# Weights of a tuned attention and feed-forward kernel placed at multiples of 512 bytes

## The chip, the cores and the metric

The kernel runs on one core of one Trainium2 chip. Its time is the device time of one execution in microseconds, taken as the median of several runs. On a core, TensorE multiplies matrices (PE in the profile, and PEld for the loading of its standing operand), VectorE (DVE), ScalarE (ACT) and GpSimd (POOL) work element by element, and SyncE (SP) mostly starts DMAs. SBUF, the memory that all of them work in, has 128 partitions; an address here is a byte offset inside a partition, the same in all 128. TensorE writes its results to PSUM, in 8 banks of 2048 bytes a partition.

## What is computed

8192 tokens (4 sequences of 2048) with 256 features each pass one layer: gated linear attention inside chunks of 32 tokens, a layer norm, a feed-forward part with integer weights, and a second layer norm.

```python
Q, K, V = x @ W_q.T, x @ W_k.T, x @ W_v.T
decay = sigmoid(log_decay[0])
mask = where(diff >= 0, decay ** diff, 0)         # 32 x 32, diff = row - column
S = einsum('bncd,bnkd->bnck', Qc, Kc) * mask      # inside each chunk of 32 tokens
O = einsum('bnck,bnkd->bncd', S, Vc).reshape(B, T, D)
out = sigmoid(x @ W_g.T) * O @ W_o.T + x
h = layernorm(x + out)
f = (silu(h @ (w_gate/127).T) * (h @ (w_up/127).T)) @ (w_down/127).T   # 256 -> 768 -> 256
y = layernorm(h + f)
```

## The kernel before

The tokens are worked on in 16 blocks of 512. W_q and W_k are first multiplied into one matrix m, so that a score is a product of x·m with x. The work is spread as a pipeline over the loop of line 1103: while one block is in its feed-forward part, the next ones are in attention. The order of the instructions on each engine is written out by hand: `in_turn` (line 115) keeps an instruction at its place in the program's order.

TensorE is fed by two kinds of products. In one kind the result has its features on the partitions: the weight is the **standing** operand (128 rows by 128 columns, loaded into the array beforehand) and 512 tokens stream past as the **moving** operand. In the other kind the result has its tokens on the partitions: 128 tokens stand, and a weight of 256 columns moves.

To get near float32 accuracy from quicker formats, numbers are split. In the attention products (lines 442 to 542) a weight and a token tile each come in three parts, `hi`, `lo` and `gap`, all in the format fp32r, and one product becomes three: hi with hi and lo with lo, then, after ScalarE has scaled the bank (line 533), gap with gap. `feature_major` (the matmul of line 492) makes the gate's and y's products this way, p_g and p_y: weights wg and m stand. `token_major` (line 514) makes p_v and p_o: weights wv and wo move. In the feed-forward part (`ffn_up`, line 870, matmul at line 881) the integer weights fg and fu stand in two exact copies, fp32r (hi) and fp16 (lo), against the two parts of the normed tokens, hT_hi and hT_lo. In its second half the parts of the hidden values, u_hi and u_lo, stand, and the weight fd moves (line 736; 955 and 1315 for the last blocks). The very last block's up products are partly done in two halves of 256 columns. Plain float32 products are used in the first block (lines 578, 599, 620, 769) and throughout for the chunk scores (line 654) and the values (line 690, where the masked scores sT move past v).

Where a tile lies follows from its pool. `tile_pool` calls take space in the order in which they are written, each pool gives space to its tags in the order of their first use, and each tag is rounded up to a multiple of 32 bytes. 16512 bytes in front are taken by the program. Then come the pools `const` (weights, masks and other things that stay), `setup`, `xin`, `work`, `norm`, `moved`, `acts`, `sums`, `small`, and last `tiny`, which holds tiles of one or a few columns. Before the change the first tile of const is `top`, 36 bytes rounded to 64, and in the middle of const stand `diff` and `chunk_mask` with 128 bytes each. The places of the tiles that TensorE reads are these, worked out from the sizes and the order:

| tiles | start before | past a multiple of 512 |
|---|---|---|
| wg, wv, wq, wk, wo (2048 each; wg, wv, wo later hold their gap parts, wq and wk hold m's hi and lo) | 16576 to 24768 | 192 |
| ident, m (m's gap) | 26816, 27328 | 192 |
| sT_0, sT_1 | 29632, 30656 | 448 |
| wg_hi, wg_lo, wv_hi, wv_lo, wo_hi, wo_lo | 31680 to 41920 | 448 |
| fg_hi, fg_lo, fu_hi, fu_lo, fd_hi, fd_lo | 43968 to 68544 | 448 |
| all tiles of tokens (xT, yT, v, hT, u, x and go parts) | from 73216 on | 0 |

Chunks inside a tile lie a multiple of 512 bytes apart, except in fg_lo and fu_lo, where 128 columns of fp16 are 256 bytes.

Of the kernel before, what the change touches and what calls it, by code (L numbers as in the profile page):

```python
# [47 lines left out]
F32 = mybir.dt.float32  # L48
F32R = mybir.dt.float32r
F16 = mybir.dt.float16  # L50
I32 = mybir.dt.int32
# [3 lines left out]
P = 128  # L55
CHUNK = 32
# [3 lines left out]
NG = TB // P  # L60
# [16 lines left out]
def kernel(  # L77
# [20 lines left out]
    NB = NT // TB  # L98
    assert NB > 3

    const = ctx.enter_context(tc.tile_pool(name="const", bufs=1))
    setup = ctx.enter_context(tc.tile_pool(name="setup", bufs=2))
    xin = ctx.enter_context(tc.tile_pool(name="xin", bufs=2))
# [8 lines left out]
    tiny = ctx.enter_context(tc.tile_pool(name="tiny", bufs=1))  # L112
    psum = ctx.enter_context(tc.tile_pool(name="psum", bufs=8, space=bass.MemoryType.PSUM))

    def in_turn(ins):
        tc.keep_in_program_order(ins)

    def bank(name):
        return psum.tile([P, TB], F32, tag="ps", name=name)
# [33 lines left out]


    n_pieces = sum(w.shape[0] * w.shape[1] // (P * TB) for w in (ffn_gT, ffn_uT, ffn_dT))
    top = const.tile([P, n_pieces], F32, tag="top", name="top")
    decay = tiny.tile([P, 1], F32, tag="decay", name="decay")
    xTs, xns = {}, {}
    wg = load_w(nc.scalar, w_gT, "wg", pieces=KD)
    xTs[0] = load_xT(0, pieces=KD)  # L160
# [43 lines left out]

    ident = const.tile([P, P], F32, tag="ident", name="ident")
    make_identity(nc, ident)
    eps = tiny.tile([P, 1], F32, tag="eps", name="eps")
    nc.vector.memset(eps, EPS)
    half = tiny.tile([P, NG], F32, tag="half", name="half")
    nc.vector.memset(half, -0.5)  # L210


# [16 lines left out]

    diff = const.tile([P, CHUNK], I32, tag="diff", name="diff")
    for g in range(P // CHUNK):
        nc.gpsimd.iota(
            diff[g * CHUNK : (g + 1) * CHUNK, :],
# [1 line left out]
            base=0,  # L237
            channel_multiplier=-1,
        )
    chunk_mask = const.tile([P, CHUNK], F32, tag="chunk_mask", name="chunk_mask")  # L240
    nc.vector.tensor_scalar(chunk_mask, diff, 0.0, None, ALU.is_ge)
    table = tiny.tile([P, 1], F32, tag="table", name="table")
    in_turn(nc.scalar.activation(table, eps, AF.Sigmoid))
    bits = []
    for i in range(CHUNK.bit_length() - 1):
# [13 lines left out]
    def make_mask():  # L259
        in_turn(nc.scalar.activation(decay, decay, AF.Sigmoid))  # L260
        power = decay
        for i, (bit, factor) in enumerate(bits):
            in_turn(
                nc.vector.scalar_tensor_tensor(factor, bit, power, factor, ALU.mult, ALU.add)
            )
            in_turn(nc.vector.tensor_tensor(chunk_mask, chunk_mask, factor, ALU.mult))
            if i < len(bits) - 1:
                square = tiny.tile([P, 1], F32, tag=f"power_{i}", name=f"power_{i}")
                in_turn(nc.vector.tensor_tensor(square, power, power, ALU.mult))
                power = square  # L270

# [31 lines left out]

    def wide_counter():

        wide = const.tile([P, top.shape[1]], F32, tag="wide", name="wide")
        in_turn(nc.vector.tensor_scalar(wide, top, EXACT, None, ALU.is_gt))
        ones = tiny.tile([P, 1], F32, tag="ones", name="ones")
        nc.vector.memset(ones, 1.0)

        def count_wide():
            pw = bank("pw")[:1, : top.shape[1]]
            in_turn(nc.tensor.matmul(pw, lhsT=ones, rhs=wide, start=True, stop=True))
            count = tiny.tile([1, 1], F32, tag="count", name="count")
            in_turn(nc.vector.tensor_reduce(count, pw, mybir.AxisListType.X, ALU.add))
            return count

        return count_wide
# [687 lines left out]

    weight_parts(wg, "wg", ("wg_hi", "wg_lo"))
    make_mask()
    back_to_silu()
    sg, gate = attn_gate(0)  # L1010
# [59 lines left out]
    y_rest()  # L1070
    look_up(range(6, n_pieces))
    count_wide = wide_counter()
    gate = g_rest(hold=True)
    hs[1], out_rest = split_out(1, go_parts)
    hTs[0] = transpose_h(0, hs[0])
    count = count_wide()
    n_wide_early = tiny.tile([1, 1], I32, tag="n_wide_early", name="n_wide_early")
    in_turn(nc.vector.tensor_copy(n_wide_early, count))
    gate()
    x_parts, x_gaps = token_parts(xTs[3], "x_3")  # L1080
# [414 lines left out]
        nc.gpsimd.dma_start(out[tokens, :], r)  # L1495


    n_wide = tiny.tile([1, 1], I32, tag="n_wide", name="n_wide")
    in_turn(nc.vector.tensor_copy(n_wide, count))
    of_others = loaded(n_wide, [e for e in mybir.ALL_ENGINES if e != mybir.EngineType.SP])  # L1500
    wide_any = bass.RuntimeValue.of_register_unchecked(
# [71 lines left out]
```

## Time and profile before

| | us |
|---|---|
| three runs | 487.17, 487.68, 488.32; median 487.68 |
| the profiled execution | 488.06 |
| its span, first to last instruction | 486.5 |
| granted TensorE clock over the span | 0.998 of full speed |
| TensorE busy (PE) | 480.3, 4760 instructions |
| loading of standing operands (PEld) | 381.5, 4760 instructions |
| ScalarE, VectorE, GpSimd busy | 374.6, 338.1, 281.1 |
| landing of the first weight, which the first product waits for | 3.36 |

The profile's groups give a line of the kernel, an engine, an operation, its tiles as out<-in, and its shape; for a matmul the first tile after the arrow is the moving one, the second the standing one. After the bar stand the busy time in us and the mean duration of one in ns. The view of the chain gives, in order of time, a start in us, a length in us, and what ran, with a count. The list of one tile gives the least, the median and the largest duration in ns. The view of waits gives who waited for whom: us in total, times, the longest.

### The profile page before, as it was taken

The page shows a single profiled execution, that of the slowest core. Times are in us where ns is not written, and L with a number is a line of the kernel's source. Part 1 is how long each engine was busy: PE and PEld are TensorE (multiplying, and loading weights), DVE is VectorE, ACT ScalarE, POOL GpSimd, SP SyncE. Part 2 cuts the span into 40 slices and gives each one's busy share as a digit, 9 for nine tenths or more (in the row PEclk, how much of TensorE's full clock was granted, in tenths as well). Part 3 has the DMA queues.
Part 4 walks back from the last instruction along what each step waited for, and adds up shares of the span by engine and source line. Part 5 has one row for each costly group of instructions (what it writes and reads, how often), then busy time and mean ns, then how long its engine had stood idle before and what let it go on. Part 6 is the DMA issues. An engine that isn't in the chain of part 4 may idle for free.

```text
span 486.5 us, 12289 instructions
## 1 busy us (share of the span) xinstructions
PE 480.3 (99%) x4760; PEld 381.5 (78%) x4760; DVE 338.1 (69%) x795; ACT 374.6 (77%) x699; POOL 281.1 (58%) x285
## 2 busy tenths in 40 slices
PE   9999999999999999999999999999999999999995
PEld 5788787887868878687887868878687787868685
DVE  4587958777676875757777676875757777667656
ACT  4778788687887878788787887878788787786845
POOL 3835755655745556465555745656465555657764
PEclk9999999999999999999999999999999999999999
DMA  8630321221413114131311313123131211103002
GB/s 256 229 101 25 104 71 49 49 80 36 125 33 113 44 51 126 31 101 52 108 60 38 127 32 112 45 65 110 26 106 53 80 44 37 54 20 113 32 16 85
DMA packets 43323, 36.99 MB, mean 76 GB/s; under 512 B 4864, under 2 KB 39168, under 8 KB 43264
## 3 DMA queue, kind: packets, MB, share of 16 engines
q1 hardware_dynamic: 42144, 35.28, 23.6%
q10 hardware_dynamic: 1120, 0.92, 0.6%
q8 instruction: 38, 0.62, 0.6%
q14 instruction: 21, 0.17, 0.1%
HBM read 20.45 MB, written 8.39 MB: 59 GB/s over the span
## 4 chain that ended last, share of the span: by engine, by line
PE 98%; DMA 1%; DVE 0%; ACT 0%; issue 0%
PE fg L881 18%; PE fu L881 18%; PE fdn L736 15%; PE p_o L514 9%; PE p_v L514 9%; PE p_y L492 9%; PE p_g L492 9%; PE po L690 4%; PE ps L654 2%; PE fdn L955 2%; PE fdn L1315 1%; PE pg L578 1%; PE pa L769 1%; PE pv L620 1%; PE py L599 1%; DMA wg<-in_w_gT_dram 1%
## 5 line engine op out<-in xcount | busy, mean ns | idle before, releaser
L907 POOL TENSOR_TENSOR u_lo<-u,u_hi 128x512 f16<-128x512 f32 (+1 forms) x98 | 129.6, 1328 | 95.2 <-ACT u_hi L906 94.2
L901 DVE SCALAR_TENSOR_TENSOR u<-fu,s 128x512 f32<-128x512 f32 (+1 forms) x98 | 66.2, 675 | 83.6 <-ACT s L890 81.4
L890 ACT ACTIVATE s<-fg 128x512 f32<-128x512 f32 (+1 forms) x98 | 57.4, 586 | 47.5 <-PE fg L881 47.5
L906 ACT CAST u_hi<-u 128x512 fp32r<-128x512 f32 (+1 forms) x98 | 59.3, 605 | 32.8 <-DVE u L901 32.8
L881 PE MATMUL fg<-hT_hi,fg_hi 128*128 128x512 f32 (+1 forms) x196 | 72.0, 449 | 0.0
L881 PE MATMUL fu<-hT_hi,fu_hi 128*128 128x512 f32 (+1 forms) x196 | 60.2, 389 | 0.0
L881 PE MATMUL fg<-hT_lo,fg_lo 128*128 128x512 f16 (+1 forms) x196 | 58.2, 379 | 0.0
L881 PE MATMUL fu<-hT_lo,fu_lo 128*128 128x512 f16 (+1 forms) x196 | 57.4, 375 | 0.0
L473 POOL TENSOR_TENSOR go_lo<-goT,go_hi 128x512 fp32r<-128x512 f32 x30 | 44.6, 1507 | 18.1 <-ACT go_hi L472 18.1
L479 DVE SCALAR_TENSOR_TENSOR go_gap<-go_hi,goT 128x512 fp32r<-128x512 f32 x30 | 48.1, 1644 | 0.8 <-ACT go_hi L472 0.7
L473 POOL TENSOR_TENSOR x_lo<-xT,x_hi 128x512 fp32r<-128x512 f32 x30 | 37.8, 1281 | 15.5 <-ACT x_hi L472 15.5
L736 PE MATMUL fdn<-fd_hi,u_hi 128*128 128x256 f32 x312 | 45.0, 287 | 0.0
L881 PEld LDWEIGHTS fg<-hT_hi,fg_hi 128*128 128x128 f32 x196 | 35.6, 189 | 10.2
L881 PEld LDWEIGHTS fu<-hT_hi,fu_hi 128*128 128x128 f32 x196 | 36.5, 188 | 8.1
L790 DVE TENSOR_TENSOR h<-p_o,x 128x512 f32<-128x512 f32 x30 | 19.3, 685 | 32.0 <-PE p_o L514 28.2
L736 PEld LDWEIGHTS fdn<-fd_hi,u_hi 128*128 128x128 f32 x312 | 39.3, 189 | 0.3
L736 PE MATMUL fdn<-fd_lo,u_lo 128*128 128x256 f16 x312 | 38.6, 273 | 0.0
L858 POOL TENSOR_TENSOR hT_lo<-hT,hT_hi 128x512 f16<-128x512 f32 x28 | 35.4, 1287 | 4.2 <-ACT hT_hi L857 4.2
L881 PEld LDWEIGHTS <-fu_lo 128*128 128x128 f16 x196 | 19.2, 98 | 22.2
L736 PEld LDWEIGHTS <-u_lo 128*128 128x128 f16 x312 | 28.4, 98 | 4.0
L426 ACT ACTIVATE h<-h,shift_h,scale_h 128x256 f32<-128x256 f32 x52 | 27.0, 590 | 1.6 <-DVE shift_h L389 0.8
L881 PEld LDWEIGHTS <-fg_lo 128*128 128x128 f16 x196 | 13.2, 98 | 19.0 <-issue 12.8
(175 smaller groups left out, 1040.2 us busy)
## 6 DMA issues: line engine op xcount, KB each, us to landing
x<-in_x_dram SPq DMA_DIRECT2D x16, 512.0 KB, 3.8
xT<-in_xT_dram SPq DMA_DIRECT2D x15, 512.0 KB, 4.3
hT<-sq SPq DMA_DIRECT2D x224, 32.0 KB, 1.9
out_dram<-r SPq DMA_DIRECT2D x13, 512.0 KB, 3.2
out_dram<-r SPq DMA_DIRECT2D x7, 128.0 KB, 1.7
fg_int<-in_ffn_gT_dram SPq DMA_DIRECT2D x3, 256.0 KB, 7.3
fu_int<-in_ffn_uT_dram SPq DMA_DIRECT2D x3, 256.0 KB, 6.4
fd_int<-in_ffn_dT_dram SPq DMA_DIRECT2D x3, 256.0 KB, 5.5
```

The costliest lines, as they stand in the source:

```text
L426: nc.scalar.activation(r[:, g, :], r[:, g, :], AF.Identity, bias=shift[:, g : g + 1], scale=scale[:, g : g + 1],)
L473: in_turn(nc.gpsimd.tensor_tensor(lo[:, k, :], t[:, k, :], whole, ALU.subtract))
L479: nc.vector.scalar_tensor_tensor(gap[:, k, :], whole, -WHOLE, t[:, k, :], ALU.mult, ALU.add)
L492: nc.tensor.matmul(pb, lhsT=a[kind][:, k, i * P : (i + 1) * P], rhs=b[kind][:, k, :], start=kind + k == 0, stop=True, skip_group_check=True,)
L514: nc.tensor.matmul(pb[:, j * D : (j + 1) * D], lhsT=b[kind][:, k, g * P : (g + 1) * P], rhs=a[kind][:, k, :], start=kind + k + j == 0, sto ...
L736: product = nc.tensor.matmul(pb[:, j * D : (j + 1) * D], lhsT=part[:, g * P : (g + 1) * P], rhs=w, start=(i == 0), stop=(i == len(terms) - 1),
L858: nc.gpsimd.tensor_tensor(in_order[1], whole, in_order[0].bitcast(F32), ALU.subtract)
L881: product = nc.tensor.matmul(pb, lhsT=w[kind][:, dc, hc * P : (hc + 1) * P], rhs=hT[kind][:, dc, cols], start=(kind == kinds[0] and dc == ...
L890: in_turn(nc.scalar.activation(s, pg, AF.Silu, scale=SCALE / H_UP))
L901: nc.vector.scalar_tensor_tensor(u, pu, U_UP / H_UP, s, ALU.mult, ALU.mult)
L906: in_steady_turn(nc.scalar.copy(hi, u))
L907: in_steady_turn(nc.gpsimd.tensor_tensor(lo, u, hi.bitcast(F32), ALU.subtract))
```

## The change

One more pool, `lead`, is opened in front of `const`. The twelve tiles of at most 16 bytes that were in `tiny` (decay, eps, half, table, four powers, ones, count, n_wide_early, n_wide) are taken from `lead`. The four small tiles of const whose sizes are no multiple of 512 (top, diff, chunk_mask, wide) are taken from `tiny`, behind all other pools. No instruction, size or order is changed.

```diff
+    lead = ctx.enter_context(tc.tile_pool(name="lead", bufs=1))
     const = ctx.enter_context(tc.tile_pool(name="const", bufs=1))
...
-    top = const.tile([P, n_pieces], F32, tag="top", name="top")
-    decay = tiny.tile([P, 1], F32, tag="decay", name="decay")
+    top = tiny.tile([P, n_pieces], F32, tag="top", name="top")
+    decay = lead.tile([P, 1], F32, tag="decay", name="decay")
...
-    eps = tiny.tile([P, 1], F32, tag="eps", name="eps")
+    eps = lead.tile([P, 1], F32, tag="eps", name="eps")
...
-    half = tiny.tile([P, NG], F32, tag="half", name="half")
+    half = lead.tile([P, NG], F32, tag="half", name="half")
...
-    diff = const.tile([P, CHUNK], I32, tag="diff", name="diff")
+    diff = tiny.tile([P, CHUNK], I32, tag="diff", name="diff")
...
-    chunk_mask = const.tile([P, CHUNK], F32, tag="chunk_mask", name="chunk_mask")
+    chunk_mask = tiny.tile([P, CHUNK], F32, tag="chunk_mask", name="chunk_mask")
...
-    table = tiny.tile([P, 1], F32, tag="table", name="table")
+    table = lead.tile([P, 1], F32, tag="table", name="table")
...
-                square = tiny.tile([P, 1], F32, tag=f"power_{i}", name=f"power_{i}")
+                square = lead.tile([P, 1], F32, tag=f"power_{i}", name=f"power_{i}")
...
-        wide = const.tile([P, top.shape[1]], F32, tag="wide", name="wide")
+        wide = tiny.tile([P, top.shape[1]], F32, tag="wide", name="wide")
...
-        ones = tiny.tile([P, 1], F32, tag="ones", name="ones")
+        ones = lead.tile([P, 1], F32, tag="ones", name="ones")
...
-            count = tiny.tile([1, 1], F32, tag="count", name="count")
+            count = lead.tile([1, 1], F32, tag="count", name="count")
...
-    n_wide_early = tiny.tile([1, 1], I32, tag="n_wide_early", name="n_wide_early")
+    n_wide_early = lead.tile([1, 1], I32, tag="n_wide_early", name="n_wide_early")
...
-    n_wide = tiny.tile([1, 1], I32, tag="n_wide", name="n_wide")
+    n_wide = lead.tile([1, 1], I32, tag="n_wide", name="n_wide")
```

## Prediction

> **What bounds the kernel now.** I read the page first: the share of each engine, then the chain that ended last, then the waits. TensorE is busy from end to end at the full granted clock, the chain lies on it, and no multiplication waits except the first warm-up one.
>
> ```profile
> span 486.5 us, 12289 instructions
> PE 480.3 (99%) x4760; PEld 381.5 (78%) x4760; DVE 338.1 (69%) x795; ACT 374.6 (77%) x699; POOL 281.1 (58%) x285
> ...
> PEclk9999999999999999999999999999999999999999
> ...
> PE 98%; DMA 1%; DVE 0%; ACT 0%; issue 0%
> ```
>
> ```profile
> PE pi L197 <- PEq L1558: 1.0, 1, 1.0
> ```
>
> So time changes only if a multiplication (PE) or a weight load (PEld) takes another time, or if something that is hidden today comes out. The other engines wait for TensorE or for each other; those waits cost nothing.
>
> Busy time of TensorE does not tell its pace, since matmuls overlap in their pipeline. The chain of waits does: there a piece is the distance from its first start to the next piece's start, so the piece divided by its count is the pace.
>
> ```profile
> 19.79 1.88 PE p_v L514 x16
> ...
> 61.32 1.82 PE p_v L514 x16
> ...
> 90.74 1.84 PE p_v L514 x16
> 92.58 1.83 PE p_g L492 x8
> ...
> 97.15 1.84 PE p_o L514 x16
> ...
> 100.89 5.43 PE fdn L736 x48
> ...
> 130.05 5.47 PE fdn L736 x48
> ```
>
> The two fdn lines say that one block of 512 tokens takes 29.16 us (130.05 less 100.89). The p_g line gives 1.83/8 = 229 ns for an fp32r multiplication of 512 columns; p_v and p_o at 1.84/16 give 115 ns for 256 columns. The reader should note the first three lines: the same sixteen instructions on the same addresses took 1.88, 1.82 and 1.84 us, that is 117.5, 113.8 and 115 ns each. There are two paces for one and the same instruction, and the block that it stands in, not its address, goes with which one it gets.
>
> **What the change moves, and by how much.** No instruction, wait, queue or DMA is added, removed or moved; only byte offsets within a partition change. In front of the const pool 16512 bytes are taken. Before, `top` (36 bytes, rounded to 64) stands there, so wg, wv, wq, wk, wo, ident and m start at 192 past a multiple of 512; their space is reused for the gap parts and for m's hi and lo. Behind `diff` and `chunk_mask` (128 bytes each) everything stands at 448: sT, wg_hi to wo_lo, and the hi and lo of fg, fu and fd. After, twelve tiles of 32 bytes stand in front: 16512 + 384 = 16896 = 33 x 512. With diff, chunk_mask, top and wide gone to the back, every const tile is a multiple of 512 long and starts at 0. The pools behind them start at 71680 as before and the tokens' tiles were at 0 already, so they do not move. So 192 and 448 become 0, for weights, and nothing else changes that TensorE reads in the loop but sT (448 to 0).
>
> **Standing weights (line 492, and 881).** Does a load at 0 take another time than one at 448 or 192? The rows already hold both: in the products over features the standing operand is a weight, in those over tokens (736) it is a token tile at 0.
>
> ```profile
> L736 PEld LDWEIGHTS fdn<-fd_hi,u_hi 128*128 128x128 f32 x312 | 39.3, 189 | 0.3
> L881 PEld LDWEIGHTS fu<-hT_hi,fu_hi 128*128 128x128 f32 x196 | 36.5, 188 | 8.1
> L881 PEld LDWEIGHTS fg<-hT_hi,fg_hi 128*128 128x128 f32 x196 | 35.6, 189 | 10.2
> L736 PEld LDWEIGHTS <-u_lo 128*128 128x128 f16 x312 | 28.4, 98 | 4.0
> L881 PEld LDWEIGHTS <-fu_lo 128*128 128x128 f16 x196 | 19.2, 98 | 22.2
> ...
> L492 PEld LDWEIGHTS p_y<-x_hi,m_hi 128*128 128x128 f32 x60 | 11.0, 188 | 2.3
> ```
>
> u_hi at 0 takes 189 ns, fg_hi and fu_hi at 448 take 189 and 188, m_hi at 192 takes 188; u_lo and fu_lo (at 448 or 192, by its chunk) take 98 each. Price of this part: 0. Its cover is wide as well: behind a 512-column multiplication there are 229 ns for a load, so even 20 ns more would stay hidden.
>
> **Moving weights (lines 514, 736, 955, 1315).** Here the weight streams past a standing token tile. The last block of the feed-forward part is done by halves, so that the same shape, 256 columns, is there with an aligned moving operand:
>
> ```profile
> L881 PE MATMUL fu<-hT_hi,fu_hi 128*128 128x256 f32 x8 | 1.6, 278 | 0.0
> L881 PE MATMUL fu<-hT_lo,fu_lo 128*128 128x256 f16 x8 | 1.5, 273 | 0.0
> ...
> L514 PE MATMUL p_v<-wv_hi,x_hi 128*128 128x256 f32 x120 | 18.9, 280 | 0.0
> ...
> L514 PE MATMUL p_v<-wv_lo,x_lo 128*128 128x256 f32 x120 | 18.6, 277 | 0.0
> ...
> L736 PE MATMUL fdn<-fd_lo,u_lo 128*128 128x256 f16 x312 | 38.6, 273 | 0.0
> ```
>
> These are durations with the pipeline's depth in them; what counts is their difference. With hT_hi moving at 0: 278 ns. With wv_hi and wv_lo moving at 448: 280 and 277. In fp16, 273 at 0 and 273 for fd_lo at 448. One tile's own list gives the spread:
>
> ```profile
> L881 PE MATMUL fu<-hT_hi,fu_hi x196: 276/393/398, 47.1 to 475.5; 128*128 128x512 f32 x188, 128*128 128x256 f32 x8
> ```
>
> ```profile
> L514 PE MATMUL p_v<-wv_hi,x_hi x120: 276/276/384, 19.6 to 413.0; 128*128 128x256 f32 x120
> ```
>
> The shortest is 276 ns with the moving operand at 0 and 276 at 448, so both offsets reach the quick pace. Price of this part: 0 by these rows. The wait-free 512-column products keep their moving operand (tokens at 0) and lose only the offset of the next load: 0.
>
> **The rest.** The start of the kernel waits 3.36 us for wg from memory, which now lands at 0 instead of 192. The queue that carries the weights (q10) moved 0.92 MB for 0.6% and the one with the aligned tokens (q1) 35.28 MB for 23.6%: 1.53 against 1.49 MB for each per cent, no handicap that alignment could take away. 0, and not over 0.1 us either way. chunk_mask, diff, eps, half and the powers are read by VectorE and ScalarE, which have slack; if that cover were gone, the 64 mask multiplications of 32 partitions would have to grow by 16 ns each to make 1 us, and no row suggests that they do. The value products (po, line 690) take sT as moving operand; it moves by 64 bytes. Their rows hold one offset only, so I bound them by the two paces above, 2% apart around 1.84: of 16 blocks at 1.09 in the chain, 17.4 us, that is 0.35 us either way, and take 0, as the 448 and 0 of the rows above agree.
>
> **The sum.** The profiled execution took 488.06 us, its span 486.5 with 1.56 around it; the median of the three runs is 487.68, 0.38 below it. The sum of the parts is 0, so the forecast is the median, 487.7. About 0.2% (1.0 us) is what a measurement of this kernel can tell from no change; the three runs spread over 1.15.
>
> **What the skill's pages would make of it.** The 229 ns above are not the 216 that fp16 takes (in the chain the fp16 pairs of line 881 stand at 0.43 us). The Trainium skill, "TensorE: Matmul & The Clock Gate", section "Back-to-back issue gap", has a warm multiplication at N/2.4 + 2.5 ns, 215.8 and 109.2 ns for 512 and 256 columns, whatever the type. By that rule the fp32r excess would be something a change could remove, and the forecast would be that of the third rival below. The same page, "Step-by-step: what each phase is for", says that loading the next weights takes no read bandwidth from the running multiplication. By that rule the first two rivals below cost nothing; the pages do not account for two paces, and the trace shows them.
>
> **The rivals.** *Faster: the groups settle at the quick pace.* The slow pace may be a collision of the moving stream with the next load, and with equal offsets the two may fall out of each other's way at once. A block has 48 products of line 514: 1.84 + 0.93 + 1.84 + 0.94 = 5.55 us in the chain, 115.6 ns each. At 113.8 that saves 48 x 1.8 = 0.09 us. The 24 fp32r products of fdn have a median duration of 281 against a least of 276; at most 24 x 5 = 0.12. Together 0.21 us for a block, 15 blocks, 3.1 us: 484.6. For it: two paces exist and cost real time. Against it: both paces occur at 448, at 192 (p_o's gap part takes 0.94 for 8, the slow pace, p_v's 0.93) and at 0.
>
> *Slower: equal offsets collide.* In front of every 256-column product the moving weight starts 448 or 192 past the grid and the standing token at 0; after the change both start at 0, a pairing that no steady group of this trace has in fp32r. If it ties the groups to the slow pace, line 514 loses 48 x (117.5 - 115.6) = 0.09 us for a block and fdn up to 12 x 5 = 0.06: 0.15 x 15 = 2.3 us, 490.0. It decides from 0.07 us a block on (1.0 us), that is half of it. For it: the pairing is new, and nothing here shows it harmless. Against it: the stream reads 1024 bytes while the load reads 512, so each passes over the other's offsets whatever the start, and 448 and 192 behave alike.
>
> *Much faster: the whole fp32r excess is misalignment.* 736 products of 512 columns would gain 229 - 216 = 13 ns and 1120 of 256 columns 278 - 273 = 5 (the durations above): 9.6 + 5.6 = 15.2 us, 472.5. Against it: the 512-column ones have their moving operand at 0 already and still take 229.
>
> The 512-column groups read 1.83 to 1.84 us for 8 throughout; if their pace too were dealt anew, 92 groups by 0.01 is 0.9 us either way, which widens the two first rivals but does not decide them.
>
> **How the numbers follow.** No effect over 0.2%: 0.56, since every offset pair that the rows hold agrees within 1 to 3 ns of 280. Faster, the groups' pace: 0.22. Slower, the same mechanism's other side: 0.20. The much faster one: 0.02. That makes faster 0.24, same 0.56, slower 0.20. The likeliest case alone spans 486.9 to 488.5. The range for 8 in 10 takes in three quarters of each rival's price: 487.7 - 2.4 = 485.3 and 487.7 + 1.8 = 489.5.
>
> **What would show it.** Right: the load rows stay at 188 to 189 and 98, fdn at 5.43 to 5.47, p_v and p_o at 1.84, p_g at 1.83, a block at 29.2. Wrong towards faster: p_v and p_o at 1.82 and fdn below 5.40. Wrong towards slower: p_v and p_o at 1.88, or loads longer than 189. A p_g or p_y other than 1.83 would say that the standing weight's offset matters after all, and wg landing after other than 3.36 us that the DMA's does.

## The result, and the profile after

The changed kernel takes 490.12 us (median of six runs, 489.80 to 491.29), the kernel before 487.75 (six runs, 487.17 to 488.32). The ratio is 1.0055, with a 95% interval from 1.0041 to 1.0069: slower, by 2.4 us. The forecast was 487.7, with a range up to 489.5; the slower rival had said 490.0. The profiled execution took 490.27 us with a span of 488.7, against 488.06 and 486.5 before. One execution of the kernel before, timed beside the last experiment, ran at 0.655 of the clock and took 685.95 us; it enters no comparison here.

The page of the changed kernel reads as before, with 2.2 us more on TensorE:

```profile
span 488.7 us, 12289 instructions
...
PE 482.5 (99%) x4760; PEld 384.0 (79%) x4760; DVE 337.8 (69%) x795; ACT 375.8 (77%) x699; POOL 281.5 (58%) x285
...
PEclk9999999999999999999999999999999999999999
...
PE 99%; DVE 0%; ACT 0%; issue 0%
```

The clock is the same, the count of instructions is the same, nothing new stands in the chain. So the products themselves have become slower. The chain of waits in the stretches that the prediction showed (start us, length us, what):

```profile
18.82 1.90 PE p_v L515 x16
...
60.44 1.90 PE p_v L515 x16
...
90.09 1.90 PE p_v L515 x16
91.99 1.84 PE p_g L493 x8
...
96.58 1.90 PE p_o L515 x16
...
100.37 5.52 PE fdn L737 x48
...
129.78 5.52 PE fdn L737 x48
```

The first three lines were 1.88, 1.82 and 1.84 us before; now all are 1.90, or 119 ns for each of sixteen products. The group p_v (120 ns) and the group fdn (5.52 against 5.43 and 5.47) have grown, p_g hardly (1.84 against 1.83). One block takes 29.41 us (129.78 less 100.37), where it took 29.16.

The lists of single tiles (least/median/largest duration in ns) and the group of loads show the same from the other side:

```profile
L515 PE MATMUL p_v<-wv_hi,x_hi x120: 274/282/386, 18.7 to 414.8; 128*128 128x256 f32 x120
```

```profile
L737 PEld LDWEIGHTS fdn<-fd_hi,u_hi x312: 187/192/192, 70.6 to 429.0; 128*128 128x128 f32 x156
```

```profile
L515 PEld LDWEIGHTS p_v<-wv_lo,x_lo 128*128 128x128 f32 x120 | 16.5, 190 | 0.0
```

The median of wv_hi's products was 276 ns and is 282. The load of u_hi, which runs beside a product that streams fd, had a median of 188 and has 192, so here the load and the stream lengthen together. Before, its list read:

```profile
L736 PEld LDWEIGHTS fdn<-fd_hi,u_hi x312: 187/188/192, 71.4 to 427.1; 128*128 128x128 f32 x156
```

From here on I use one number per group: the distance from each product's start to the start of the next product on TensorE, read from the trace and summed over the whole run for all products of a group. Such sums leave out no part of TensorE's time up to the start of the last product, so their differences add up to that of the spans (2.2 us).

| group | before, us | after, us | difference |
|---|---|---|---|
| p_v, 360 products | 42.01 | 43.28 | +1.27 |
| p_o, 360 | 42.19 | 43.14 | +0.95 |
| fdn, first place (line 736 before), 624 | 71.04 | 71.73 | +0.69 |
| fdn, last blocks (955 and 1315) | 16.42 | 16.59 | +0.17 |
| p_g, 180 | 41.97 | 42.13 | +0.16 |
| p_y, 180 | 44.21 | 44.18 | -0.04 |
| first products, pg (line 578), 8 | 4.79 | 3.96 | -0.83 |
| all others | | | -0.17 |
| sum | | | +2.20 |

The products in which a weight moves lose 3.08 us; the products in which it stands lose about nothing. The -0.83 is the kernel's start: the eight first products read anything between 3.5 and 4.9 us in the profiles of this case, with no order by layout, so it is the scatter of one execution and no part of the change. Without it the two profiled executions would lie 3.0 us apart; the 2.4 us between the medians has an interval from 2.0 to 3.4.

The single distances say what has happened. Before, of the steps from one fp32r product of p_v to the next, 60% lay under 116 ns (mostly at 113 and 114) and 28% between 116 and 119. After, 9% lie under 116, and 68% at 119 or more, the most frequent value being 120 ns. This is neither of the two paces known from before but a third, slower one.

### The profile page after: what moved, and what is told of

Read it like the earlier page. It is cut to its first block, busy times and chain, and to the rows that moved or that the text cites. A ratio compares the mean times of both kernels' runs of the same rounds, so it can differ in the third digit from the quotient of the medians.

```text
span 488.7 us, 12289 instructions
## 1 busy us (share of the span) xinstructions
PE 482.5 (99%) x4760; PEld 384.0 (79%) x4760; DVE 337.8 (69%) x795; ACT 375.8 (77%) x699; POOL 281.5 (58%) x285
## 4 chain that ended last, share of the span: by engine, by line
PE 99%; DVE 0%; ACT 0%; issue 0%
PE fg L882 18%; PE fu L882 18%; PE fdn L737 15%; PE p_v L515 9%; PE p_o L515 9%; PE p_y L493 9%; PE p_g L493 9%; PE po L691 4%; PE ps L655 2%; PE fdn L956 2%; PE fdn L1316 1%; PE pg L579 1%; PE pv L621 1%; PE pa L770 1%; PE py L600 1%; PE pi L198 1%
## 5 line engine op out<-in xcount | busy, mean ns | idle before, releaser
L389 POOL TENSOR_SCALAR minus_out<-rstd_out 128x4 f32<-128x4 f32 x12 | 2.7, 223 | 44.3 <-DVE rstd_out L387 44.3
```

## The experiments

The theory after the result: what counts is where the moving weight starts **relative to the token tile that is loaded meanwhile**. I call d the offset of the weight minus the offset of the token tile, in bytes past a multiple of 512. Before, d was 448 or 192 everywhere; after, it is 0. Rivals: the absolute address of the moving weight (0 is bad in itself); the other kilobytes in which the weights now lie; the standing weights; the small tiles, now behind everything.

All layouts below are made from the changed kernel in one way: fd, wo and wv get pools of their own, behind const and ahead of the tokens' pools, and an unused tile in front of a pool shifts it. No instruction changes.

```diff
+    md = ctx.enter_context(tc.tile_pool(name="md", bufs=1))
+    mo = ctx.enter_context(tc.tile_pool(name="mo", bufs=1))
+    mv = ctx.enter_context(tc.tile_pool(name="mv", bufs=1))
+    homes_of = {"wv": mv, "wo": mo, "fd": md}
+
+    def home(tag):
+        return homes_of.get(tag[:2], const)
...
-        t = const.tile([P, k, n], w.dtype, tag=name, name=name)
+        t = home(name).tile([P, k, n], w.dtype, tag=name, name=name)
```

**Other kilobytes, same offsets.** With these pools alone every offset stays 0.

> All offsets as in the changed kernel (standing weights, moving weights and tokens at 0), but the moving weights wv, wo and fd have pools of their own behind the standing ones, so all of them lie some kilobytes elsewhere. If only the offset within 512 bytes counts, this is the changed kernel again: 490.1 us, p_v and p_o of 16 products at 1.90 to 1.92. If whole kilobytes count, the time differs from 490.1 by over 0.5.

Measured: 490.53 us, ratio 1.0065 (1.0048 to 1.0081). p_v 43.31, p_o 43.15, fdn's first place 71.73: the sums of the changed kernel to 0.03 us, in other kilobytes. Its chain:

```profile
149.82 1.90 PE p_v L523 x16
...
156.32 1.90 PE p_o L523 x16
```

So this shift by kilobytes changed nothing, and this kernel is a fair base for the others.

**Moving weights back at 448, standing weights at 0.**

```diff
+    pad_md = ctx.enter_context(tc.tile_pool(name="pad_md", bufs=1))
+    pad_md.tile([P, 112], F32, tag="pad_md", name="pad_md")
     md = ctx.enter_context(tc.tile_pool(name="md", bufs=1))
...
+    pad_tok = ctx.enter_context(tc.tile_pool(name="pad_tok", bufs=1))
+    pad_tok.tile([P, 16], F32, tag="pad_tok", name="pad_tok")
     setup = ctx.enter_context(tc.tile_pool(name="setup", bufs=2))
```

> Standing weights and tokens stay at 0, the moving weights wv, wo, fd go back to 448. Theory A (a moving weight and a standing token tile that start at the same offset collide) and theory B (a moving weight that starts at 0 is slow by itself): the 3.1 us that lines 514, 736, 955 and 1315 lost come back, 487.0 us, p_v of 16 at 1.84 or below. Theory C (the standing weights or the small tiles do it): 490 us as the changed kernel.

**The reverse: standing weights at 448, moving weights at 0.**

```diff
+    pad_st = ctx.enter_context(tc.tile_pool(name="pad_st", bufs=1))
+    pad_st.tile([P, 112], F32, tag="pad_st", name="pad_st")
     const = ctx.enter_context(tc.tile_pool(name="const", bufs=1))
+    pad_md = ctx.enter_context(tc.tile_pool(name="pad_md", bufs=1))
+    pad_md.tile([P, 16], F32, tag="pad_md", name="pad_md")
     md = ctx.enter_context(tc.tile_pool(name="md", bufs=1))
```

> Standing weights go back to 448, moving weights and tokens at 0. Theories A and B: still slow, 490 to 491 us, p_v of 16 at 1.90 to 1.92. Theory C: 487.7 us, as before.

Measured: moving weights at 448 give 487.91 us (487.0 was expected), ratio 1.0007 (0.9997 to 1.0017); standing weights at 448 give 491.17, ratio 1.0074 (1.0057 to 1.0091). The loss goes with the moving weights, but for a rest of 0.5 us in p_o. In the chain of the first of the two, p_v is quick again and fdn too, while p_o stays at 1.89:

```profile
100.22 5.44 PE fdn L749 x48
...
265.35 1.83 PE p_v L527 x16
...
271.75 1.89 PE p_o L527 x16
```

In the second both are slow:

```profile
149.88 1.91 PE p_v L527 x16
...
156.37 1.92 PE p_o L527 x16
```

The p_o that stays slow (sum 42.68; 42.19 before) is not explained by its own d, which is that of p_v. Its steps stand at 117 and 118 ns (78% of them), the known slow pace, not at 120. It comes back below.

**Distance or address.** All weights stay at 0, as in the changed kernel; instead every tile of tokens goes to 64. That makes d = -64, that is 448, with no weight at 448.

```diff
+    pad_tok = ctx.enter_context(tc.tile_pool(name="pad_tok", bufs=1))
+    pad_tok.tile([P, 16], F32, tag="pad_tok", name="pad_tok")
     setup = ctx.enter_context(tc.tile_pool(name="setup", bufs=2))
```

> All weights at 0 as in the changed kernel, but every token tile is moved to 64, so that a moving weight again starts 448 past a standing token tile (mod 512). Theory A: p_v and p_o of 16 back at 1.84 or below, about 487 us. Theory B: they stay at 1.90 to 1.92 and the time at 490.

Measured: 487.26 us, ratio 0.9998 (0.9988 to 1.0008). The sums are those of before: p_v 42.01 (42.01 before), p_o 42.14 (42.19), fdn 71.04 (71.04), p_g 41.97 (41.97), p_y 44.22 (44.21). The chain can be laid beside that of the prediction piece by piece:

```profile
90.27 1.84 PE p_v L525 x16
...
96.68 1.84 PE p_o L525 x16
...
100.42 5.43 PE fdn L747 x48
...
129.57 5.47 PE fdn L747 x48
```

This settles the main question: with the weights at multiples of 512 the loss is gone once the tokens stand 64 bytes further. Not the address counts, but the distance: weights at 448 with tokens at 0 and weights at 0 with tokens at 64 are one distance at two places, and their sums agree within 0.05 us. (Distance 0 was run only with the tokens at 0.) It clears the small tiles as well: in this kernel they lie as the change put them, and nothing is lost. (They were not moved alone.)

**Which distances are bad?** Three layouts with a different d for each weight. Standing weights (S), wv, wo and fd at 32, 64, 128, 256; at 128, 256, 320, 384; at 256, 32, 480, 64. The edit of the first; the others differ in the sizes of the unused tiles and the order of the pools:

```diff
+    pad_st.tile([P, 8], F32, tag="pad_st", name="pad_st")
     const = ctx.enter_context(tc.tile_pool(name="const", bufs=1))
...
+    pad_mv.tile([P, 8], F32, tag="pad_mv", name="pad_mv")
+    mv = ctx.enter_context(tc.tile_pool(name="mv", bufs=1))
...
+    pad_mo.tile([P, 16], F32, tag="pad_mo", name="pad_mo")
+    mo = ctx.enter_context(tc.tile_pool(name="mo", bufs=1))
...
+    pad_md.tile([P, 32], F32, tag="pad_md", name="pad_md")
+    md = ctx.enter_context(tc.tile_pool(name="md", bufs=1))
...
+    pad_tok.tile([P, 64], F32, tag="pad_tok", name="pad_tok")
```

> Tokens at 0. Standing weights at 32, wv at 64, wo at 128, fd at 256: three distances of a moving weight from a standing token tile in one run. So far distance 0 gives p_v 43.3, p_o 43.1, fdn 88.3 us over the run, with most products at 120 ns, and 448 or 192 gives 42.0, 42.2, 87.5 with most at 113 or 118. If only equal offsets within 512 bytes collide, all three groups stand near the lower numbers. If the offset counts within 256 bytes, fdn (256) shows 120 ns and 88.3; within 128 bytes, p_o (128) too; within 64 bytes, all three.

> Tokens at 0. Standing weights at 128, wv at 256, wo at 320, fd at 384. Within 512 bytes alone: all three near 42.0, 42.2, 87.5. Within 256: p_v at 43.3 with 120 ns, the other two low. Within 128: p_v and fdn slow. Within 64: all slow.

> Tokens at 0. Standing weights at 256, wv at 32, wo at 480 (32 below the grid), fd at 64. If a collision needs the same 64 bytes, 32 and 480 stand between: wv at 32 still partly meets the token's first line and p_v lies above 42.0; if it needs the same 32 bytes or the exact start, p_v and p_o are at 42.0 and 42.2. fdn at 64 as in the run with wv at 64: 87.5 unless 64 bytes are the period.

Measured, one time each beside 487.87 for the kernel before on the same chip: 491.00, 490.93 and 488.37 us. Single times of kernels whose start alone scatters by over 1 us say little; the sums of the groups say more, and stand in the table below. Two more layouts filled the gaps: S, wv, wo, fd at 64, 96, 160, 160 and at 224, 416, 352, 352. For the second of these:

```diff
+    pad_st.tile([P, 56], F32, tag="pad_st", name="pad_st")
     const = ctx.enter_context(tc.tile_pool(name="const", bufs=1))
...
+    pad_md.tile([P, 32], F32, tag="pad_md", name="pad_md")
+    md = ctx.enter_context(tc.tile_pool(name="md", bufs=1))
+    mo = ctx.enter_context(tc.tile_pool(name="mo", bufs=1))
...
+    pad_mv.tile([P, 16], F32, tag="pad_mv", name="pad_mv")
+    mv = ctx.enter_context(tc.tile_pool(name="mv", bufs=1))
...
+    pad_tok.tile([P, 24], F32, tag="pad_tok", name="pad_tok")
```

> Tokens at 0. Standing weights at 64, wv at 96, wo and fd at 160. So far a moving weight costs most at 0 or 256 (p_v 43.3), at 64 some 0.9 more than at 448 or 192 (42.0). If the cost only falls away close to 192 within 256, wo and fd at 160 lie between (p_o 42.2 to 43.0) and wv at 96 near 42.9. Standing weights have cost nothing at 0, 256, 192 and 448 (p_g 42.0, p_y 44.1 to 44.2) and 0.4 and 0.6 at 32 and 128; at 64 I expect the same 42.4 and 44.8.

> Tokens at 0. Standing weights at 224, wv at 416 (160 within 256), wo and fd at 352 (96 within 256). If the offset counts within 256 bytes, p_v here relates to p_o of the run with wo at 160, and p_o to p_v of the run with wv at 96, each by the same excess over 42.0 and 42.2. Standing at 224: between 0 and 42.4 for p_g, as 32 from either of two good places.

Measured: 492.45 and 491.74 us, beside 488.22 before on the same chip. All sums in us, by d modulo 256; where a distance was run more than once the row gives the least and the largest. Each layout moves several weights at once, and a sum can hold some tenths that come from its neighbours: p_o's at 192 differ by 0.5 us.

| d modulo 256 | p_v | p_o | fdn, first place | p_g | p_y |
|---|---|---|---|---|---|
| 0 | 43.24-43.33 | 43.11-43.49 | 71.55-71.79 | 41.97-42.13 | 44.16-44.21 |
| 32 | 42.67 | | | 42.38 | 44.88 |
| 64 | 42.91 | 42.79 | 71.23 | 42.29 | 44.80 |
| 96 | 43.60 | 43.39 | 71.82 | | |
| 128 | | 42.98 | 71.17 | 42.35 | 44.77 |
| 160 | 43.33 | 42.92 | 71.26 | | |
| 192 | 42.01-42.22 | 42.14-42.68 | 70.73-71.04 | 41.97-42.04 | 44.09-44.22 |
| 224 | | 42.97 | | 42.33 | 44.80 |

In p_v, p_o and fdn the weight moves, in p_g and p_y it stands. Three readings:

First, the period. wv at 256 behaves as at 0; the tile's list is that of the changed kernel for the same tile, to the nanosecond. Here the layout with wv at 256:

```profile
L533 PE MATMUL p_v<-wv_lo,x_lo x120: 279/283/283, 19.6 to 415.9; 128*128 128x256 f32 x120
```

And the changed kernel, d = 0:

```profile
L515 PE MATMUL p_v<-wv_lo,x_lo x120: 279/283/283, 19.1 to 415.3; 128*128 128x256 f32 x120
```

With 192 and 448 alike in the kernel before, this says that the effect repeats every 256 bytes, for the two pairs that were run. The gap parts of wv and wo give the same: 14.14 and 14.34 us at 192 before, 14.17 and 14.34 at 448 in the layout with the tokens at 64.

Second, the effect is graded. None of the clean cases that the expectations set out came true as a whole: for a moving weight each of the seven distances other than 192 costs something in every group that was run at it, from 0.1 to 1.6 us against before, and in p_v 96 costs more than 0. wv at 32 (median 279) and at 96 (median 282, largest 287) lie between and above:

```profile
L533 PE MATMUL p_v<-wv_lo,x_lo x120: 277/279/281, 18.9 to 413.6; 128*128 128x256 f32 x120
```

```profile
L531 PE MATMUL p_v<-wv_lo,x_lo x120: 278/282/287, 20.1 to 417.4; 128*128 128x256 f32 x120
```

Nor does an excess carry from one group to another at the same d: at 160, p_v lost 1.3 us and p_o 0.7. And a slower stream does not need a longer load. With fd at 352 (96) fdn's sum is the largest in the table, 71.82 us, and the load of u_hi keeps its 188 ns:

```profile
L753 PEld LDWEIGHTS fdn<-fd_hi,u_hi x312: 187/188/193, 70.6 to 430.4; 128*128 128x128 f32 x156
```

Third, the kernel before lay at 192, the best of the distances that were run, in all its groups. For standing weights 0 is as good, which is why p_g and p_y hardly changed. At 32, 64, 128 and 224 they do: 0.3 to 0.4 us in p_g and 0.55 to 0.7 in p_y. The chain of the layout with S at 128 shows p_g at 1.86, where 1.83 stood:

```profile
267.14 1.91 PE p_v L533 x16
269.05 1.86 PE p_g L511 x8
```

**Is it the load beside the stream?** In fdn the products come as a run of fp32r ones and a run of fp16 ones. If the cause is an fp32r load during an fp32r stream, it must vanish when the two alternate: each fp32r stream then has the shorter fp16 load beside it. The edit changes only the order in which the products are added up, in the first place of fdn; the last blocks keep theirs. Run twice, with fd at 0 and with fd at 448, all else at 0.

```diff
-        pairs = list(zip(parts, ws))[:: -1 if g % 2 else 1]
-        return [term for part, w in pairs for term in zip(part, w)]
+        pairs = [list(zip(part, w)) for part, w in zip(parts, ws)]
+        return [term for both in zip(*pairs) for term in both]
```

> All offsets 0, and the products of fdn at line 736 alternate between the fp32r and the fp16 part (hi, lo, hi, lo) instead of six and six; nothing else is changed. If what costs time is the fp32r load that runs beside the moving weight, an fp32r product now has no fp32r load beside it (the next standing tile is fp16), and the time of this line does not depend on fd's offset: it rises for the change of type, by some 0.55 us a block to 78 us, in this run and in the one with fd at 448 alike, within 0.2. If the moving weight at 0 is slow whatever is loaded, this run is 0.7 to 1.0 us above the other at that line.

> As the run before this one, with fd at 448 and all else at 0. The same time at line 736 within 0.2 us by the theory of the load beside the stream; 0.7 to 1.0 us less by the rival that the moving operand's own start counts. p_v and p_o keep 43.3 and 43.1 in both.

Measured: fdn's first place 75.82 us at 0 and 75.79 at 448, where without alternation it was 71.73 and 70.76. The difference between the offsets, 0.97 us, has become 0.03. The level was missed (about 78 expected, alternating costs 4 to 5 us and not 6 to 7), the equality was met. The last blocks, not alternated, are a control inside the same two runs. Their groups, with fd at 0:

```profile
L964 PE MATMUL fdn<-fd_hi,u_hi 128*128 128x256 f32 x48 | 7.6, 294 | 0.0
```

and with fd at 448:

```profile
L968 PE MATMUL fdn<-fd_hi,u_hi 128*128 128x256 f32 x48 | 7.5, 292 | 0.0
```

294 against 292 ns, and as sums of that place 11.10 and 11.00 us: there the offset still acts. The times, 496.41 and 495.69, are those of a slower order and not to be compared with before.

That the effect needs an fp32r load beside the stream is not shown by this, because another limit may hide it. In the alternating order an fp32r and an fp16 product together take 247 ns from start to start, at both offsets. In the order of before they take 113 to 122 and 109 to 110 ns, 232 at most. Something slower than either pace thus governs the pair, and the 3 ns a pair that are at stake (0.97 us over 312 pairs) could lie under it. The load of u_hi is not undisturbed there either: its median is 203 ns with fd at 0 and 201 at 448, the longest of all layouts. The chain shows the level, with fd at 0:

```profile
131.40 5.92 PE fdn L745 x48
```

and with fd at 448:

```profile
130.75 5.91 PE fdn L749 x48
```

What all layouts do show is that products with fp16 on both sides do not react: most steps from one fd_lo product to the next stand at 109 to 110 ns whatever fd's offset.

**The p_o that stayed slow, and a layout to beat both.** With moving weights at 448 p_o had stayed at 118 ns, while fdn was quicker than before (70.76 against 71.04). What differed from before in front of p_o were the standing weights, wg and m at 0 (and sT and ident, which lie in the same pool). So: wg, m and all moving weights back at 448, only fg and fu at 0.

```diff
+    up_pool = ctx.enter_context(tc.tile_pool(name="up_pool", bufs=1))
+    pad_st = ctx.enter_context(tc.tile_pool(name="pad_st", bufs=1))
+    pad_st.tile([P, 112], F32, tag="pad_st", name="pad_st")
     const = ctx.enter_context(tc.tile_pool(name="const", bufs=1))
...
+    homes_of = {"wv": mv, "wo": mo, "fd": md, "fg": up_pool, "fu": up_pool}
```

> Tokens at 0, all moving weights and wg and m at 448 (as good as before), and only the standing weights of the up products, fg and fu, at 0, where the run with all standing weights at 0 read fg 98.2 and fu 73.1 against 98.4 and 73.3 before, and fdn 87.2 against 87.5. If p_o's 0.5 us more in that run came from wg and m at 0, this one has p_o at 42.2 and takes 487.0 us, faster than before by 0.1 to 0.2%. If it came from fu at 0, whose products stand just ahead of p_v and p_o, p_o is at 42.7 again and the time is that of before, 487.6.

Measured: p_o is back at 42.15, p_v 42.04, fdn 70.73, the time 486.75 us against 487.18 on the same chip, ratio 0.9993 (0.9984 to 1.0003). The chain:

```profile
100.55 5.43 PE fdn L750 x48
...
265.27 1.83 PE p_v L528 x16
...
271.67 1.84 PE p_o L528 x16
```

So the half microsecond of p_o came from the place of wg and m, or of sT and ident, which moved with them; all are operands of other products (p_g's stand between p_o's in the chain). fdn's gain of 0.3 us stayed. The layout with the tokens at 64 has every distance of this one but that of fg and fu, and has fdn at 71.04, so the gain goes with fg and fu at 0. A group can settle at 113 or at 118 ns with its own operands unmoved. The two products of fu just ahead of p_o take 231 and 227 ns where p_o's sixteen steps stay at 117 to 119, and 233 and 236 where they fall to 113 and 114 after the third. That this entry decides is inferred, not shown. The layout has the lowest time of all, but its interval holds 1, so nothing that was run is shown to be faster than the kernel before.

**What stays open.** Why 192 is the quiet distance, and what of the memory or of TensorE the two reads share, is not shown; nor is why a group stays at 118 ns once it has begun so, nor whether the load beside the stream must be fp32r too. The runs fix where the effect lies and on which distance it depends, not its cause inside the chip.

## Why the prediction was wrong

**The step that failed is the one on moving weights, priced at 0.** It measured +3.08 us: p_v +1.27, p_o +0.95, fdn +0.86. The price came from line 881's products of 256 columns, whose moving operand stood at 0 and which were as quick as those at 448. But in those rows the standing weight was at 448. I had matched the offset of one operand and not the pair. No row of before had the two operands at the same offset in fp32r, and the prediction said so, under the slower rival; then it let rows without that pair set the price.

**The argument against the slower rival failed.** "Each passes over the other's offsets whatever the start" is refuted by the eight distances: the start decides, by up to 1.6 us in one group. "448 and 192 behave alike" was a true reading with the wrong conclusion: they behave alike because they lie 256 apart, which is the period, not because offsets don't count.

**That rival came nearest.** It was right that the new pair of offsets slows the moving groups. It was not right that equal offsets are what collides: every distance other than 192 slowed them, and 96 at least as much as 0. It put the loss at 0.15 us a block (0.09 for line 514, 0.06 for fdn) and the time at 490.0; over 15 blocks the sums give 0.148 for line 514 and 0.057 for fdn, 0.205 in all (3.08 us against its 2.3), and the time is 490.12. The term that was too small is line 514's: the rival let the groups fall to the slow pace seen before, 117.5 ns, and they fell to 120. That 490.0 stands so close to 490.12 is partly luck: the median before and the 3.08 us of the groups would make 490.8, within the interval of the measured difference. The rival had been given 0.20, and its price went into the range by three quarters only, which put the upper end at 489.5, 0.6 us below what came. Nothing in the profile had bounded it, so its whole price belonged in the range, which would then have ended at 490.0, still 0.1 short.

**Standing weights at 0: right.** p_g and p_y moved by +0.16 and -0.04 us, the loads of fg, fu and m's hi read 190, 188 and 188 ns (189, 188 and 188 before). But the reason given, that the loads of different products take the same time at 0, 192 and 448, was too weak: at 32, 64, 128 or 224 the same step would have cost about a microsecond in p_g and p_y together. The cover of 229 ns was no protection either: at 32 and 64 the loads of wg and m still read 187 to 189 ns (medians), and the products slowed all the same. The price held since 0 happens to be a good distance for standing weights; that was luck.

**The rest at 0: right.** The value products changed by -0.08 us. The warm-up products, with the wait for wg behind them, read 3.23 against 3.38 us, and the first products after them scatter by more than that whatever the layout.

**The faster rival and the much faster one** are excluded. Equal offsets did not settle the groups at the quick pace but at a third one. And no layout brought the fp32r products down to the fp16 ones: the quickest steady steps stayed at 113 ns, where those of fp16 stand at 109 to 110.

**The signs named beforehand pointed the right way:** p_v and p_o at 1.88 and loads over 189 ns were to mean slower; they read 1.90, and 190 (x_lo) and 192 (u_hi). The sign for standing weights, a p_g other than 1.83, was seen in other layouts: 1.86 at 128.

## What to carry to other kernels

In a stream of fp32r products the offset of a tile can be judged only by pairs, that of the moving operand against that of the standing one loaded meanwhile: "aligned" is no virtue by itself, and the same alignment for all operands made one of the bad pairs here. When moving a buffer changes a tuned kernel by half a per cent, compare the steps from product to product first, and try an unused tile in front of one side. Which side matters: 64 bytes in front of the tokens took the loss away here (d = 448), while d = 64 cost p_v 0.9 us. A row prices a new case only if it has the whole pair of operands in common with it, and a rival that no row excludes belongs in the range with its whole price.

## What the runs showed of the hardware

- An fp32r product of 256 columns has at least three steady paces in these programs, which differ in addresses alone, at full granted clock: 113 to 114, 117 to 118 and 120 ns. Which ones occur depends on the start of the moving weight minus that of the standing tokens (0: mostly 120; 192: 113 and 118), alike at 0 and 256 and at 192 and 448. Which of the occurring ones a group takes can change without its own operands moving (p_o's sum 42.15 or 42.68 us).
- At distance 0 the loads that run beside lengthen with the stream: 188 to 192 ns for u_hi. At 96 the stream is as slow and the load stays at 188.
- Products with fp16 on both sides keep 109 to 110 ns at every offset that was run. With fp16 loads beside fp32r streams the offset of fd changed 75.8 us by 0.03, but at a slower pace, 247 ns a pair, that may hide it.
- The Trainium skill, "TensorE: Matmul & The Clock Gate", section "Step-by-step: what each phase is for", gives the array two independent read ports, one for the streaming operand and one for the load. The 113 against 120 ns at one and the same clock depend on the offset between the two operands, so in fp32r the two reads are not independent in time.
